# When the fp8 adjacency blocks of a two-layer graph kernel are made, and with which operations

## The chip, the cores and the metric

The kernel runs on one core of one Trainium2 chip. The metric is device microseconds (us) of one execution. The engines are TensorE (PE: matmuls, and PEld: its weight loads), VectorE (DVE), ScalarE (ACT), GpSimd (POOL) and SyncE (SP, which here only issues DMAs). Each takes its own instructions in the order in which they were written, and waits where an operand isn't there yet.

## The reference, cut to what matters

`x` is 3327 x 512 and `adj` is 3327 x 3327 with entries 0 and 1, both in float32.

```
# layer 0: two attention layers over the graph
for l in range(2):
    Wh, Ws = split(x @ W[l])                      # 512 columns each
    a      = softmax(Wh @ Ws.T, axis=-1) * adj
    x      = leaky_relu(a @ Wh + x, 0.01)
x = layernorm(x_in + x)
# layer 1: a binary linear layer, gathered over the graph
xw  = max(sign(x), 0) @ sign(weight).T            # small integers
out = layernorm(x + relu(adj @ xw))
```

So `adj` is used three times: as a mask in each of the two attention layers, and as the left operand of the last product `adj @ xw` (the aggregation). For that last product the kernel keeps `adj` in fp8 blocks that it makes on the way, while the mask is in SBUF anyway.

## The kernel before, in words

**Tiling.** The 3327 rows are padded to 26 tiles of 128, or 13 pairs (NQ = 13). A step is a pair (g, q): 256 target rows by 256 source rows, 169 steps per attention layer. All big products are done on 2 x 2 quarters with seven multiplications instead of eight, which needs sums of quarters.

**Scores.** The scores are made for 512 targets and 256 sources at a time: a unit is (c, q), made in two halves, `ahead` lists the halves. A unit is seven products in the order Z1, X2, Z6, Y5 (first half) and Z7, Y3, Z4 (second half), each two float32 matmuls of 128x256 (L586). ACT copies Z1, Z6, Y5, Z7 (p1, u2, p5, u3; L603) and Z4 (L638) out of PSUM; DVE adds (L613 after X2, L628 after Z7, L634 after Y3) and keeps a running maximum (L654, L656). The three PSUM banks of the scores go round: in the built program a unit's Z1 takes the bank that L613 of the unit before has read, its X2 mostly the one that L634 has read, its Y5 then the one that L638 has read. For the last pair of targets (c = 6, one half only) there are plain products instead (`direct`, L643).

**Attention steps.** The loop `for v in range(-LOOK - 4, len(steps))` with LOOK = 30 writes the whole order of the work down. In iteration v stand: half-unit v + 30 of the scores; for step v + 3 the shift by the column maximum (L739, DVE) and the exponential (L744, L745, ACT); for step v + 2 the running sum (L750) and the mask, `masked` (L755, DVE), then four sums of quarters on POOL (L793 to L796); for step v the seven products with the values (`values`, L820). Inside an iteration every piece of work carries a number from about 0 to 1, and the pieces are written in the order of these numbers. So iterations up to v = -4 hold scores alone, from v = 0 on PE alternates scores and values, and after v = 151 there are values alone. When a group g is done, `take_out` and `finish` (L846 to L928) follow over the next steps. Around v = -4, and later in the last third of each odd group, stands `column_max` (L687 to L707), which turns the running maxima into the shift `off` that L739 needs.

**Blocks.** `load_adj` brings a 256 x 256 float32 mask (256 KB, tag `adj`, 4 buffers) on SP's queue, in the iteration four before its step; where the mask has padding, POOL clears that first (L719, L721), and SP's load waits for it. For half of the steps in each attention layer, those with q of the layer's parity, the mask is also made into seven fp8 blocks of 128 x 128 (tile `ab`, tag `adj_b`, 2 buffers): three plain quarters and the four sums S1 to S4 of quarters. In iteration k - 2 of a step k, DVE makes the sums (`halved_sums`, L775), ACT casts the plain quarters (`halved`, L761 and L762), DVE tests that every entry is 0 or 1 (`exact`, L784, in place); an iteration later POOL issues the store to DRAM (`keep_blocks`, L778). Which mask is made in which iteration is set by the dictionary `blocks`: steps of groups 0 to 8 in their own iteration, the 28 (layer 0) or 24 (layer 1) steps of groups 9 to 12 spread over iterations of the other parity of groups 0 to 8, each with a second load of its mask.

**Aggregation.** At the end `load_aggregate` reads the blocks back and `aggregate` (L1134) multiplies them; `BLOCKS` says which of the seven is used by which product.

Of the kernel before, what the change touches and what calls it, by code (L numbers as in the profile page):

```python
# [15 lines left out]
ALU = mybir.AluOpType  # L16
# [3 lines left out]
P = 128  # L20
# [10 lines left out]
def kernel(  # L31
# [8 lines left out]
    nc = tc.nc  # L40
    N, D = x.shape
    L = w_stack.shape[0]
# [4 lines left out]
    NQ = NT // 2  # L47
    assert NT % 2 == 0 and D == 4 * P

    def rows(t):  # L50
        return min(P, N - t * P)
# [11 lines left out]
    def half_cols(g):  # L63

        return g * HW, min(HW, N - g * HW)
# [9 lines left out]
    LOOK = 2 * NQ + 4  # L75
# [14 lines left out]
    cnt = keep.tile([P, NQ * NQ], F32, name="cnt")  # L90
# [13 lines left out]
    adj_d = tc.dram_tile([NQ, P, NQ, 7, P], F8, name="adj_d")  # L104
# [5 lines left out]
    def load_rows(eng, dst, src, r):  # L110

        cut = r - r % 16
        engines = eng if isinstance(eng, tuple) else (eng,)
        if cut:
            engines[0].dma_start(out=dst[:cut], in_=src[:cut])
        if cut < r:
            engines[-1].dma_start(out=dst[cut:r], in_=src[cut:r])
# [437 lines left out]
    def attention(l, att):  # L555
# [3 lines left out]
        steps = [(g, q) for g in range(NQ) for q in range(NQ)]  # L559
        ahead = [(c, q, s) for c in range(NC) for q in range(NQ) for s in range(2)]  # L560
        sc, top, total, off, adj, acc, gs, xs, ch = ({} for _ in range(9))
# [152 lines left out]
        def load_adj(g, q):  # L714
            i0, n = half_cols(g)
            at = att.tile([P, 2, HW], F32, tag="adj", bufs=4, name=f"adj_{l}_{g}_{q}")
            adj[g, q] = at
            if n < HW:
                nc.gpsimd.memset(at[:, :, n:], 0.0)  # L719
            if rows(2 * q + 1) < P:  # L720
                nc.gpsimd.memset(at[:, 1], 0.0)  # L721
            if rows(2 * q + 1) == P:
                nc.sync.dma_start(
                    out=at[:, :, :n],
                    in_=adjT[2 * q * P : (2 * q + 2) * P, i0 : i0 + n].rearrange(
                        "(a p) i -> p a i", p=P
                    ),
                )
                return
            for a in range(2):  # L730
                j = 2 * q + a
                load_rows(
                    nc.sync, at[:, a, :n],
                    adjT[j * P : j * P + rows(j), i0 : i0 + n], rows(j),
                )

        def shift(g, q):
            s = sc[g, q]
            nc.vector.tensor_tensor(s, s, off[g].to_broadcast([P, 2, HW]), ALU.subtract)  # L739

        def exponential(g, q):
            if q == 0:
                total[g] = att.tile([P, 2, HW], F32, tag="total", name=f"total_{l}_{g}")
                nc.scalar.activation(total[g], sc[g, q], AF.Exp)  # L744
            nc.scalar.activation(sc[g, q], sc[g, q], AF.Exp)  # L745

        def running(g, q):

            if q > 0:
                nc.vector.tensor_tensor(total[g], total[g], sc[g, q], ALU.add)  # L750

        def masked(g, q):

            s = sc[g, q]
            nc.vector.tensor_tensor(s, s, adj[g, q], ALU.mult)  # L755
            sums(g, q, s)

        def halved(g, q):

            at, t = adj[g, q], adj[g, q, "b"]  # L760
            nc.scalar.copy(t[:, 0:2], at[:, :, :P], saturate=False)  # L761
            nc.scalar.copy(t[:, 2], at[:, 1, P:], saturate=False)  # L762

        def halved_sums(g, q):
            at = adj[g, q]
            t = adj[g, q, "b"] = att.tile(
                [P, 7, P], F8, tag="adj_b", bufs=2, name=f"ab_{l}_{g}_{q}"
            )
            a11, a21, a12, a22 = (at[:, k, ts(i, P)] for k in range(2) for i in range(2))
            s1, s2, s3, s4 = (t[:, i] for i in range(3, 7))  # L770
            for to, a, b, op in (
                (s1, a21, a22, ALU.add), (s2, s1, a11, ALU.subtract),
                (s3, a11, a21, ALU.subtract), (s4, a12, s2, ALU.subtract),
            ):
                nc.vector.tensor_tensor(to, a, b, op, saturate=False)  # L775

        def keep_blocks(g, q):
            nc.gpsimd.dma_start(out=adj_d[g][:, q], in_=adj.pop((g, q, "b")))  # L778

        def exact(g, q):  # L780

            at = adj.pop((g, q))
            i = g * NQ + q
            nc.vector.scalar_tensor_tensor(  # L784
                at, at, 0.0, at, ALU.is_gt, ALU.not_equal, accum_out=cnt[:, i : i + 1],
            )

        def sums(g, q, s):
# [10 lines left out]
        def load_ws(g, q):  # L799
            t = att.tile([P, 4, HD], F32, tag="ws", bufs=WS, name=f"ws_{l}_{g}_{q}")  # L800
            nc.sync.dma_start(out=t, in_=ws_d[l][q])
            ws[g, q] = t
# [150 lines left out]
        else:  # L953
# [3 lines left out]
            for i in range(2 * KD):  # L957
                h, t = divmod(i, KD)
# [11 lines left out]
            n = len(steps) - end - 3  # L970
# [19 lines left out]
            laid, n = [], len(steps)  # L990
# [6 lines left out]
                early.setdefault(end + 7 + i, []).append((0.65, lambda: parts.pop(0)()))  # L997


        first = NQ * (NQ - 4)  # L1000
        mine = [i for i, e in enumerate(steps) if e[1] % L == l]
        room = [i for i, e in enumerate(steps[:first]) if e[1] % L != l][2:]
        late = [i for i in mine if i >= first]
        blocks = {i: steps[i] for i in mine if i < first}
        blocks.update(
            {room[n * len(room) // len(late)]: steps[i] for n, i in enumerate(late)}
        )
        later, after = [], []
        first_products = NQ * NQ - EARLY
        for v in range(-LOOK - 4, len(steps)):  # L1010
            u = v + LOOK

            if 0 <= v + WS - 1 < len(steps):
                load_ws(*steps[v + WS - 1])
            if 0 <= v + 4 < len(steps):
                load_adj(*steps[v + 4])
                if blocks.get(v + 4, steps[v + 4]) != steps[v + 4]:
                    load_adj(*blocks[v + 4])
            for lead, load in ((2, load_xs), (4, load_gs)):
                if 0 <= u + lead < len(ahead):  # L1020
                    c, q, h = ahead[u + lead]
                    if h == 0 and (lead == 2 or q == 0):
                        load(c, q)
            work, after = after, []
            if 0 <= v + 3 < len(steps):
                s3 = steps[v + 3]
                work += [(0.0, lambda: shift(*s3)), (0.12, lambda: exponential(*s3))]
            if 0 <= v + 2 < len(steps):
                s2 = steps[v + 2]
                work += [(0.01, lambda: running(*s2)), (0.4, lambda: masked(*s2))]  # L1030
                of = blocks.get(v + 2)
                if of:
                    work += [
                        (0.6, lambda: halved_sums(*of)), (0.62, lambda: exact(*of)),
                        (0.61, lambda: halved(*of)),
                    ]
                    after.append((0.5, lambda of=of: keep_blocks(*of)))
            if later:
                work += [(0.7, later.pop(0))]
            if 0 <= u < len(ahead):  # L1040
                work += scores(*ahead[u])
            if v >= 0:
                work += values(*steps[v])
            work += early.get(v, [])
            if last and 0 <= v - first_products < EARLY:
                p = v - first_products
                work += [(0.5, lambda i=i: aggregate(0, 0, p, i)) for i in BANKS[0]]
            for _, do in sorted(work, key=lambda e: e[0]):
                do()
            if v >= 0 and steps[v][1] == NQ - 1:  # L1050
                later += finish(steps[v][0])
            if last:
                load_products(v)
# [26 lines left out]
    EARLY = NQ - 2  # L1080
    XH = NT // 2
    BANKS = (0, 1), (2, 3), (4, 5), (6,)
    BLOCKS = 0, 1, 4, 5, 3, 6, 2
    xw, xw_tiles, xt, ah, po = {}, [], {}, {}, {}

    def load_products(v):
# [37 lines left out]
    def aggregate(g, b, p, i):  # L1124
        if p == 0 and i == BANKS[b][0]:
            pool, tag = (ps_acc, "acc") if g % 2 else (ps_ch, "ch") if b < 3 else (ps_tr, "tr")
            po[g, b] = pool.tile([P, 2, HD], F32, tag=tag, name=f"agg_{g}_{b}")
        x1, x2, t = xw[2 * p], xw[2 * p + 1], xt.get(p)
        if i < 2:
            of = (x1, x2)[i][:, :HD]  # L1130
        else:
            of = (t[:, 1], t[:, 2], t[:, 0], x2[:, HD:], t[:, 3])[i - 2]

        nc.tensor.matmul(  # L1134
            po[g, b][:, i % 2], ah[g, p][:, BLOCKS[i]], of,
            start=(p == 0 and i % 2 == 0), stop=(p == NQ - 1), skip_group_check=True,
        )
# [223 lines left out]
```

## Time and profile before

| what | value |
|---|---|
| median of 3 runs | 2616.8 us (2616.53 to 2617.85) |
| the profiled execution: time | 2613.73 us |
| its span, first to last instruction | 2611.9 us |
| PE busy | 2578.8 us, 99% of the span |
| PEld busy | 2234.7 us, 86% |
| DVE busy | 2109.5 us, 81% |
| POOL busy | 1091.7 us, 42% |
| ACT busy | 799.8 us, 31% |
| mean granted clock of TensorE | 0.999 |
| the scores' products into bank Z (L586), both layers: first and last start | 184.7 us, 2276.3 us |
| the products with the values (L820), both layers: first and last start | 276.6 us, 2471.0 us |

How to read it: "busy" is the time in which an engine has an instruction under way; a matmul's end is modelled, so that a short stall of PE can hide between two matmuls. The table of stretches gives, for each stretch, an engine's busy time and in brackets how many of its instructions fall into it; where all matmuls are alike, too low a count shows a stall better than the busy time does. A group line of the profile reads: line, engine, operation, names out<-in, partitions x elements and type, count | busy us, mean ns of one | idle time just before them and what ended it. A line of waits reads: who, at which line, waited for whom: us in total, times, longest.

### The profile page before, as it was taken

How to read it: one execution, taken by the hardware profiler on the slowest of the kernel's cores; microseconds unless marked ns; L12 is line 12 of the kernel's file. 1: busy time of each engine (PE TensorE's matmuls, PEld its weight loads, DVE VectorE, ACT ScalarE, POOL GpSimd, SP SyncE). 2: the span in 40 equal slices, each digit the busy share in tenths (PEclk: the TensorE clock that was granted, in tenths of full speed). 3: DMA queues.
4: the chain of work that ended last, by engine and by line, in shares of the span. 5: the costliest groups of instructions: out<-in, count | busy, mean ns of one | idle time of the engine just before them, and what ended most of it. 6: DMA issues, size and time to landing. Idle time of an engine off the chain costs nothing. (4 is left out here: it accounts for less than half of the span.)

```text
span 2611.9 us, 40070 instructions
## 1 busy us (share of the span) xinstructions
PE 2578.8 (99%) x12511; PEld 2234.7 (86%) x12536; DVE 2109.5 (81%) x4422; ACT 799.8 (31%) x1978; POOL 1091.7 (42%) x2025
## 2 busy tenths in 40 slices
PE   9999999999999999999999999999999999999998
PEld 7888888888888888887888888888888888888787
DVE  6754888899888996768874689989899898777976
ACT  3323332333323332221332333333333333222143
POOL 3640343444434444456662044444444444454610
PEclk9999999999999999999999999999999999999999
DMA  6855777777777877698865678777787777678775
GB/s 216 293 193 180 241 241 265 241 268 251 261 240 236 276 239 237 223 265 252 300 242 179 224 225 283 249 250 258 239 281 247 246 263 237 231 260 262 262 252 182
DMA packets 309783, 639.15 MB, mean 245 GB/s; under 512 B 35048, under 2 KB 177986, under 8 KB 308027
## 3 DMA queue, kind: packets, MB, share of 16 engines
q1 hardware_dynamic: 273868, 530.29, 62.8%
q0 software_dynamic: 35664, 106.18, 11.0%
q8 instruction: 103, 1.69, 0.3%
q14 instruction: 118, 0.96, 0.1%
q10 hardware_dynamic: 30, 0.03, 0.0%
HBM read 529.69 MB, written 106.67 MB: 244 GB/s over the span
## 5 line engine op out<-in xcount | busy, mean ns | idle before, releaser
L586 PE MATMUL pZ<-gs,xs 128*128 128x256 f32 x2496 | 636.9, 379 | 3.0 <-ACT u L603 2.8
L793 POOL TENSOR_TENSOR as<-s 128x128 f32<-128x128 f32 x338 | 162.7, 481 | 1052.6 <-DVE s L755 873.2
L586 PEld LDWEIGHTS pZ<-gs,xs 128*128 128x128 f32 x2496 | 473.0, 190 | 71.3 <-ACT u L603 6.3
L820 PE MATMUL acc<-ws,s 128*128 128x256 f32 x1352 | 402.4, 379 | 0.1
L820 PE MATMUL acc<-wh,s 128*128 128x256 f32 x1352 | 355.7, 379 | 0.7 <-DVE s L755 0.4
L820 PE MATMUL acc<-ws,as 128*128 128x256 f32 x1352 | 348.0, 380 | 4.2 <-POOL as L795 4.1
L745 ACT ACTIVATE s<-s 128x512 f32<-128x512 f32 x338 | 213.2, 631 | 394.3 <-DVE s L739 393.3
L586 PE MATMUL pY<-gs,xs 128*128 128x256 f32 x1248 | 320.8, 379 | 6.0 <-ACT p L603 6.0
L820 PEld LDWEIGHTS acc<-ws,as 128*128 128x128 f32 x1352 | 256.1, 190 | 45.7 <-POOL as L795 8.6
L820 PEld LDWEIGHTS acc<-wh,s 128*128 128x128 f32 x1352 | 256.6, 190 | 36.7 <-DVE s L755 1.9
L820 PEld LDWEIGHTS acc<-ws,s 128*128 128x128 f32 x1352 | 255.7, 190 | 35.5 <-DVE h L855 1.3
L586 PEld LDWEIGHTS pY<-gs,xs 128*128 128x128 f32 x1248 | 236.6, 190 | 40.0 <-ACT p L603 7.9
L656 DVE TENSOR_TENSOR top<-top,s 128x512 f32<-128x512 f32 x286 | 199.9, 713 | 72.9 <-ACT s L643 52.6
L739 DVE TENSOR_TENSOR s<-s,off 128x512 f32<-128x512 f32 x338 | 246.8, 730 | 0.6
L755 DVE TENSOR_TENSOR s<-s,adj 128x512 f32<-128x512 f32 x338 | 239.5, 709 | 8.6 <-DMA adj<-in_adjT_dram 0.6
L750 DVE TENSOR_TENSOR total<-total,s 128x512 f32<-128x512 f32 x312 | 230.3, 738 | 0.0
L795 POOL TENSOR_TENSOR as<-s 128x128 f32<-128x128 f32 x338 | 202.1, 598 | 26.5
L603 ACT COPY u<-pZ 128x256 f32<-128x256 f32 x312 | 115.5, 370 | 308.0 <-PE pZ L586 304.9
L820 PE MATMUL acc<-wh,as 128*128 128x256 f32 x676 | 202.5, 381 | 0.0
L794 POOL TENSOR_TENSOR s<-s 128x128 f32<-128x128 f32 x338 | 182.9, 541 | 27.4
L796 POOL TENSOR_TENSOR as<-s,as 128x128 f32<-128x128 f32 x338 | 183.0, 541 | 26.5
L628 DVE TENSOR_TENSOR s<-p,u 128x256 f32<-128x256 f32 x156 | 66.5, 427 | 137.6 <-ACT u L603 136.9
(214 smaller groups left out, 3886.8 us busy)
## 6 DMA issues: line engine op xcount, KB each, us to landing
ws<-ws_d SPq DMA_DIRECT2D x338, 512.0 KB, 3.8
xs<-xs_d SPq DMA_DIRECT2D x182, 512.0 KB, 5.7
adj<-in_adjT_dram SPq DMA_DIRECT2D x324, 256.0 KB, 4.3
xs<-xs_d SPq DMA_DIRECT2D x156, 384.0 KB, 6.2
gs_d<-gsp POOLq DMA_DIRECT2D x88, 256.0 KB, 3.1
gs<-gs_d SPq DMA_DIRECT2D x12, 1792.0 KB, 10.9
adj_d<-ab POOLq DMA_DIRECT2D x169, 112.0 KB, 3.9
ahl<-adj_d SPq DMA_DIRECT2D x78, 224.0 KB, 5.0
```

The costliest lines, as they stand in the source:

```text
L586: nc.tensor.matmul(ch[bank], xs[c, q, a][:, k], gs[c][:, b, k], start=(start and k == 0), stop=(k == 1), skip_group_check=True,)
L603: nc.scalar.copy(ch[name], ch[bank])
L656: nc.vector.tensor_tensor(top[i], top[i], t, ALU.max)
L739: nc.vector.tensor_tensor(s, s, off[g].to_broadcast([P, 2, HW]), ALU.subtract)
L745: nc.scalar.activation(sc[g, q], sc[g, q], AF.Exp)
L750: nc.vector.tensor_tensor(total[g], total[g], sc[g, q], ALU.add)
L755: nc.vector.tensor_tensor(s, s, adj[g, q], ALU.mult)
L793: nc.gpsimd.tensor_tensor(s3, a11, a21, ALU.subtract)
L794: nc.gpsimd.tensor_tensor(a21, a21, a22, ALU.add)
L795: nc.gpsimd.tensor_tensor(s2, a21, a11, ALU.subtract)
L796: nc.gpsimd.tensor_tensor(s4, a12, s2, ALU.subtract)
L820: nc.tensor.matmul(acc[g][i // 2][:, i % 2], a[i], b[i], start=(q == 0 and i % 2 == 0), stop=(q == NQ - 1), skip_group_check=True,)
```

## The change

The blocks of a step are made with other operations, at another place in the loop, and for some steps in other iterations.

- **Sums.** `halved_sums` (four DVE operations on 128 columns, two of which read or write fp8 intermediates) becomes `block_sums`, three DVE operations: the difference of the left and right halves, for both rows of quarters at once and in place in the float32 mask (L770 of the new kernel); S2 from it (L771); S4 and S1 side by side as one sum of 256 columns (L774). They read float32 alone.
- **Test.** `exact` (L790) comes ahead of the sums, and writes its unused result into four of the fp8 blocks instead of over the mask.
- **ACT.** `raw_blocks` (L765) casts two quarters an iteration earlier than before (k - 3). The other two blocks, S3 and the fourth quarter, are cast by ACT in `keep_blocks` (L782), an iteration after the sums (k - 1), just ahead of the store (L783).
- **Place.** 14 steps of each attention layer are moved into iterations of scores alone: into v + 2 = -27, -25, ..., -1. In layer 0 these are the steps (12, q) and (11, q) with even q; in layer 1 the steps (g, 11) of odd g, and (12, q) and two of (11, q). All others are made at their own step, those of groups 9 to 11 too, and no iteration makes blocks of two parities any more. The masks of the moved steps are loaded a second time (28 loads instead of 52).
- The order of the seven blocks in memory changes, and `BLOCKS` with it.

```diff
-        def halved(g, q):
-
-            at, t = adj[g, q], adj[g, q, "b"]
-            nc.scalar.copy(t[:, 0:2], at[:, :, :P], saturate=False)
-            nc.scalar.copy(t[:, 2], at[:, 1, P:], saturate=False)
-
-        def halved_sums(g, q):
-            at = adj[g, q]
+        def raw_blocks(g, q):
             t = adj[g, q, "b"] = att.tile(
                 [P, 7, P], F8, tag="adj_b", bufs=2, name=f"ab_{l}_{g}_{q}"
             )
-            a11, a21, a12, a22 = (at[:, k, ts(i, P)] for k in range(2) for i in range(2))
-            s1, s2, s3, s4 = (t[:, i] for i in range(3, 7))
-            for to, a, b, op in (
-                (s1, a21, a22, ALU.add), (s2, s1, a11, ALU.subtract),
-                (s3, a11, a21, ALU.subtract), (s4, a12, s2, ALU.subtract),
-            ):
-                nc.vector.tensor_tensor(to, a, b, op, saturate=False)
+            nc.scalar.copy(t[:, 0:2], adj[g, q][:, :, :P], saturate=False)
+
+        def block_sums(g, q):
+            at, t = adj[g, q], adj[g, q, "b"]
+            left, right = at[:, :, :P], at[:, :, P:]
+            nc.vector.tensor_tensor(left, left, right, ALU.subtract)
+            nc.vector.tensor_tensor(
+                t[:, 6], at[:, 1, P:], at[:, 0, :P], ALU.subtract, saturate=False
+            )
+            nc.vector.tensor_tensor(
+                t[:, 4:6].rearrange("p a i -> p (a i)"), at[:, 0], at[:, 1], ALU.add,
+                saturate=False,
+            )
 
         def keep_blocks(g, q):
-            nc.gpsimd.dma_start(out=adj_d[g][:, q], in_=adj.pop((g, q, "b")))
+            at, t = adj.pop((g, q)), adj.pop((g, q, "b"))
+            quarter = at.rearrange("p k (i n) -> p (k i) n", n=P)
+            nc.scalar.copy(t[:, 2:4], quarter[:, 0:4:3], saturate=False)
+            nc.gpsimd.dma_start(out=adj_d[g][:, q], in_=t)
 
         def exact(g, q):
 
-            at = adj.pop((g, q))
+            at = adj[g, q]
             i = g * NQ + q
+            junk = adj[g, q, "b"][:, 3:7].rearrange("p (k i) n -> p k (i n)", k=2)
             nc.vector.scalar_tensor_tensor(
-                at, at, 0.0, at, ALU.is_gt, ALU.not_equal, accum_out=cnt[:, i : i + 1],
+                junk, at, 0.0, at, ALU.is_gt, ALU.not_equal, accum_out=cnt[:, i : i + 1],
+                saturate=False,
             )
...
-        first = NQ * (NQ - 4)
+
         mine = [i for i, e in enumerate(steps) if e[1] % L == l]
-        room = [i for i, e in enumerate(steps[:first]) if e[1] % L != l][2:]
-        late = [i for i in mine if i >= first]
-        blocks = {i: steps[i] for i in mine if i < first}
-        blocks.update(
-            {room[n * len(room) // len(late)]: steps[i] for n, i in enumerate(late)}
-        )
+        alone = list(range(4 - LOOK, 1, 2))
+        moved = [i for i in mine if l and steps[i][1] == NQ - 2 and steps[i][0] % 2]
+        moved += [i for i in mine[::-1] if i not in moved][: len(alone) - len(moved)]
+        blocks = {i: steps[i] for i in mine if i not in moved}
+        blocks.update({i - 1: steps[j] for i, j in zip(alone, moved)})
...
             if 0 <= v + 4 < len(steps):
                 load_adj(*steps[v + 4])
-                if blocks.get(v + 4, steps[v + 4]) != steps[v + 4]:
-                    load_adj(*blocks[v + 4])
+            elif v + 4 in blocks:
+                load_adj(*blocks[v + 4])
...
-                of = blocks.get(v + 2)
-                if of:
-                    work += [
-                        (0.6, lambda: halved_sums(*of)), (0.62, lambda: exact(*of)),
-                        (0.61, lambda: halved(*of)),
-                    ]
-                    after.append((0.5, lambda of=of: keep_blocks(*of)))
+            if v + 3 in blocks:
+                work += [(0.61, lambda: raw_blocks(*blocks[v + 3]))]
+            if v + 2 in blocks:
+                of = blocks[v + 2]
+                work += [(0.6, lambda: exact(*of)), (0.62, lambda: block_sums(*of))]
+                after.append((0.4, lambda of=of: keep_blocks(*of)))
...
-    BLOCKS = 0, 1, 4, 5, 3, 6, 2
+    BLOCKS = 0, 1, 6, 2, 5, 4, 3
```

## The prediction, made before the changed kernel ran

> **What bounds the kernel now.** First the page's busy times and slices, then the stretches of 50 us, then the waits in the stretches where PE falls short, then the groups of the block work, last the order of time where the moved work will stand.
>
> ```profile
> PE 2578.8 (99%) x12511; PEld 2234.7 (86%) x12536; DVE 2109.5 (81%) x4422; ACT 799.8 (31%) x1978; POOL 1091.7 (42%) x2025
> ...
> PE   9999999999999999999999999999999999999998
> ...
> DVE  6754888899888996768874689989899898777976
> ```
>
> PE is the bound: 33.1 us of idle time in 2611.9 us. A change on DVE, ACT and DMA can only give back PE's stalls, or add some. The stretches say where they are:
>
> ```profile
> 350.00:400.00 50.00, 50.00 (x235) 43.98 (x234) 41.70 (x89) 15.12 (x40) 20.99 (x41) 1.00 0.81 278
> 400.00:450.00 50.00, 48.45 (x223) 41.41 (x222) 45.88 (x113) 15.54 (x44) 18.82 (x38) 1.00 0.72 233
> 450.00:500.00 50.00, 48.51 (x224) 42.05 (x223) 44.41 (x92) 15.18 (x40) 23.62 (x46) 1.00 0.75 242
> ...
> 750.00:800.00 50.00, 45.77 (x209) 38.81 (x208) 44.74 (x101) 14.76 (x40) 19.91 (x38) 1.00 0.69 222
> ```
>
> The first bracket counts PE's matmuls. Full stretches of layer 0 hold 233 to 235; in scores alone a unit of 28 matmuls takes 6.04 us (Z1 at 190.76 and at 196.80), 0.216 us each. Layer 0 loses 10.6 + 9.6 + 24.6 matmuls here and 1.6 in 600 to 650: 46.4 x 0.216 = **10.0 us** (busy time shows 7.4 of it). Layer 1's groups 0 to 8 show two waits of 0.6 us (near 1830 and 2150). Where values begin, 250 to 300 us is 6.6 matmuls short (1.4 us) and 1450 to 1500 7.6 (1.6 us). The end of layer 1 (2440 to 2470, PE waiting for L795) loses some 4 us, but holds no block work before or after the change. The waits from 430 to 432.2 us:
>
> ```profile
> ACT ab L761 <- DMA adj_d<-ab: 2.6, 1, 2.6
> DVE ab L775 <- DMA adj_d<-ab: 2.6, 1, 2.6
> PEld pY L586 <- ACT p L603: 1.9, 1, 1.9
> PE pY L586 <- ACT p L603: 1.5, 1, 1.5
> ```
>
> The cast L761 wants an `ab` buffer whose store, issued at 425.27, hasn't landed; behind it on ACT stands the copy p5, for which Y3 waits. The same stands at 458 and 779 us. So layer 0's stalls come from two blocks in neighbouring steps with two buffers, where `column_max` has made the first late. Over the kernel such waits are 28.6 us on DVE and 27.1 on ACT.
>
> **What the Trainium skill says.** "DMA: Bandwidth & Descriptors", section "Anatomy of one DMA — SWDGE (gpsimd) path": about 2.0 us fixed plus bytes by 436 GB/s, and a wait on a semaphore is taken by the issuing sequencer ahead of the transfer. For 112 KB that is an estimate of 2.3 us; this trace has a median of 3.9 and here about 5.9, so the trace is used. The second statement agrees: SP stands at one load with all later ones behind it. "VectorE: DVE Perf Modes", section "Mode 1× (REGULAR) — the baseline": one result a cycle, at 0.96 GHz; 256 columns are an estimate of 0.27 us, 128 of 0.13. The trace has 0.42 (L628) and 0.35, so some 0.15 to 0.2 us is fixed per operation, and fewer, wider ones save.
>
> **The change, part by part.** Block work, by form:
>
> ```profile
> L784 DVE SCALAR_TENSOR_TENSOR adj<-adj 128x512 f32<-128x512 f32 x169 | 139.8, 827 | 25.4 <-ACT ab L762 8.9 <-ACT u L603 0.5 <-DVE ab L775 0.5
> L775 DVE TENSOR_TENSOR ab<-adj 128x128 fp8e4<-128x128 f32 x338 | 118.0, 349 | 29.2 <-DMA adj_d<-ab 28.6 <-POOL as L793 0.4
> L775 DVE TENSOR_TENSOR ab<-adj,ab 128x128 fp8e4<-128x128 f32 x169 | 86.5, 512 | 0.0
> L775 DVE TENSOR_TENSOR ab<-ab,adj 128x128 fp8e4<-128x128 fp8e4 x169 | 79.3, 469 | 5.8
> ```
>
> *DVE per block.* Before: 2 x 0.349 + 0.512 + 0.469 + 0.827 + 0.078 (accumulator read) = 2.58 us. After: 0.42 (256 columns, L628's row) + 0.35 + 0.42 + 0.91 = 2.10. An fp8 result of 256 columns and a strided one in place are not in the trace: between 0.35 and 0.54 each, so 1.95 to 2.35; I take 2.1. ACT: 0.401 + 0.296 becomes 2 x 0.40, on an engine at 31%. Saved on DVE: 169 x 0.48 = 81 us, worth nothing by itself under PE.
>
> *(a) Stores.* Blocks now come two steps (12 us) apart, so a buffer is wanted again after 24 us; a store of 3.9 to 6 us is long done. Layer 0's 10.0 us go, and DVE in groups 0 to 8 falls from 90% to about 75% (in layer 0, 20.5 x 2.58 us per 26 steps of 6.05 us become 14 x 2.1). What is next: ACT's cast in `keep_blocks` waits for L770; from 0.62 of a step to 0.4 of the next are 4.7 us, less 1.3 for L790 and L770, so DVE may be 3 us late. I leave 0.8 us. **-9.2 us** (bounds -10.0 and -6). *(b)* Layer 1's two waits (exponential behind a late L739): **-1.2** (0 to -2.2).
>
> *(c) Start of layer 0's scores.* The first moved mask, (12, 12), is padded. SP has had the second unit's operands in early; now this mask stands ahead of them (they were ahead of the last input loads before). Its second piece waits for POOL's clearing, and POOL is busy with stores until 186.90:
>
> ```profile
> 186.36 0.54 POOL L417 DMA_DIRECT2D ws_d<-t  x1
> ```
>
> Clearing (0.11 + 0.32) to 187.4, issues of 0.38 each on SP, the last piece at 188.2, landing about 3 us later: 191.3. L765 stands between u2 and p5 on ACT: cast to 191.7, p5 to 192.1, and Y3, begun at 189.03 before, waits 3.1 us. The second unit's first operand (issued 188.6, landing 3.8 to 5 us) is needed at 193.9: covered, else more. **+3.1** (2.0 to 5). *(d)* Layer 1's first mask, (1, 11), isn't padded: issued at 1399.7 when PE leaves the buffer, landed at 1404, Y3 begins at 1404.85. **+0.3** (0 to 1.5).
>
> *(e) Scores alone.* Per unit of 6.04 us DVE has 3 x 0.42 + 2 x 0.71 + 2.1 = 4.8 us. Order: L634, block, two maxima, L613; the next Z1 wants that L613 some 2.5 us later. No stall; 896 KB and 256 KB per unit fit too.
>
> *(f) Where values begin* DVE has no gap from 262.21 on:
>
> ```profile
> 262.62 0.42 DVE L634 TENSOR_TENSOR s<-pY,u 128x256 f32<-128x256 f32 x1
> ...
> 268.74 0.69 DVE L739 TENSOR_TENSOR s<-s,off 128x512 f32<-128x512 f32 x1
> 269.35 0.42 DVE L628 TENSOR_TENSOR s<-p,u 128x256 f32<-128x256 f32 x1
> 269.68 0.42 DVE L634 TENSOR_TENSOR s<-pY,u 128x256 f32<-128x256 f32 x1
> ...
> 271.28 0.68 DVE L739 TENSOR_TENSOR s<-s,off 128x512 f32<-128x512 f32 x1
> ```
>
> The blocks (11, 2) and (11, 0) now come right behind the two L634. The first moves the second L634 to 272.2, and X2, which began at 270.19 on its release, waits 2.1 us. With the second, L739 of 271.28 is 4.2 us late, with it the exponential, then a cast (0.4) and u2 on ACT: Z7, at 273.17 before, begins at about 277.4. X2 of the next unit waits 0.7 us. In all 4.8 us instead of 1.4: **+3.4**. In layer 1, likewise with (11, 9) and (11, 7), 4.2 instead of 1.6: **+2.6**. Bounds of both together 3 to 8 us (the cheapest and dearest block, twice each).
>
> *(g) Groups 9 to 11* get 14 and 10 blocks that they had not. From v = 126 a step is 4.7 us; DVE has 26.2 us in 1050 to 1080 and gets 3 x 2.1: over 30 by 2.5 us, and slack follows (5.9 in 1080 to 1090). **+0.6** (0 to 4). (h) 24 loads fewer, the new order of blocks: 0, under the slack of SP's queue; with that cover gone 0.4 us of issue each.
>
> Sum: -9.2 - 1.2 + 3.1 + 0.3 + 3.4 + 2.6 + 0.6 = **-0.4 us**: 2613.7 becomes 2613.3 in the profiled execution. That execution lies 3.1 us under the median of the runs, so 2616.4.
>
> **The rivals.** *R1, faster:* (a) and (b) as above, but the starts cost half or less, because landings in (c) come at the short end and PE regains at one place what it lost at another (waits in (f) overlap instead of adding): -10.4 + 3 = -7.4, 2609.4. For it: 55 us of waits on stores go; against: DVE's unbroken row from 262 us. *R2, slower:* ACT's cast in `keep_blocks` becomes the wait. Where DVE is more than 3 us behind its place, the cast blocks u2 or p5 as L761 did; at some 8 places (ends of odd groups, group 10) by 1 us: -0.4 + 8, 2624.4. It decides from 3 us of lateness; for it, (g)'s full stretches and L745's waits of up to 5.9 us for L739; against, DVE at 75%. *R3:* the change doesn't do what it says: stalls stay, since late DVE and not the stores made them, and the starts cost: 2626. Against it: the named waits.
>
> **How the numbers follow.** Forecast 0.45, R1 0.38, R2 0.14, R3 0.03. A measurement of this kernel can tell 0.2%, 5.2 us: faster 0.38, same 0.45, slower 0.17. The forecast's own range is 2611.6 to 2622. For 8 in 10 the range goes to 2606.5 (a fifth of R1 is left out, 0.08) and 2623 (over half of R2 and R3, 0.10).
>
> **What would show it.** Right: matmul counts of 233 and more around 430, 455 and 775 us, no waits on `adj_d<-ab`; a gap of PE near 189 us behind the cast; 2 + 2 us on X2 and Z7 near 272; DVE busy lower by about 80 us. Wrong: no gap at those starts (R1), or PE waiting for p5 or u2 behind the second cast of ACT (R2), or stalls still near 430 (R3).

## The result, and the profile after

The changed kernel takes 2622.4 us (median of 15 runs, 2617.9 to 2624.9), the kernel before 2615.7 us in the same series (15 runs, 2612.0 to 2617.9): a ratio of 1.0025, interval 1.0019 to 1.0032. It is slower by 0.25%, 6.7 us, where 2616.4 was forecast. The time lies 0.4 us above the forecast's own range (2611.6 to 2622) and inside the wider one (2606.5 to 2623), but the sum of the prediction (-0.4 us) is wrong by 7 us: the kernel was to stay where it was, and it got slower.

First the page's busy times of the changed kernel, then its stretches of 50 us at the places that the prediction named. The columns are PE, PEld, DVE, ACT and POOL (busy us, and number of instructions), granted clock, DMA share, GB/s.

```profile
PE 2584.1 (99%) x12536; PEld 2240.1 (85%) x12536; DVE 2110.5 (81%) x4253; ACT 813.7 (31%) x1978; POOL 1186.0 (45%) x2023
```

```profile
150.00:200.00 50.00, 47.61 (x213) 41.27 (x212) 27.48 (x63) 13.16 (x36) 20.94 (x39) 0.97 0.62 211
...
250.00:300.00 50.00, 43.79 (x198) 36.92 (x197) 39.93 (x101) 18.13 (x50) 10.88 (x18) 1.00 0.75 253
...
400.00:450.00 50.00, 50.00 (x233) 44.03 (x232) 43.92 (x98) 16.83 (x42) 23.31 (x40) 1.00 0.77 267
450.00:500.00 50.00, 50.00 (x234) 43.99 (x233) 40.98 (x76) 14.59 (x37) 23.70 (x42) 1.00 0.72 232
...
750.00:800.00 50.00, 50.00 (x234) 43.98 (x234) 44.62 (x92) 15.08 (x39) 24.24 (x42) 1.00 0.70 233
...
1450.00:1500.00 50.00, 45.70 (x201) 38.59 (x200) 36.63 (x96) 19.29 (x54) 4.13 (x11) 0.97 0.78 262
```

The stalls on stores are gone: 233 or 234 matmuls near 430, 460 and 780 us, where 223, 224 and 209 stood. The starts pay for it: against full stretches of 233, 20 matmuls are missing where layer 0's scores begin, 35 where its values begin (6 of them before the change too), and 32 where layer 1's values begin (7 of them before too). And there is something new in the last columns: a granted clock of 0.97 in two of these stretches.

**Stages.** Since ACT's copies out of PSUM stand in the same order in all these kernels, one and the same copy can be looked up in two traces, and the growth of the difference between its two start times tells in which stage time was lost. The next table does that for every kernel of this study, as us lost (+) or gained (-) against the trace before; the head of a column gives its stage in the time of the kernel before. What is left out (204 to 258) is 0.0 to 0.2 in all. Each row comes from one execution; stages that an edit does not touch differ by up to 0.9 us from row to row.

| kernel | 0 to 12 | 12 to 204: scores begin, layer 0 | 258 to 338: values begin | 338 to 1040: groups 0 to 8 | 1040 to 1268: groups 9 to 12 | 1268 to 1468: scores begin, layer 1 | 1468 to 1542: values begin | 1542 to 2266: groups 0 to 8 | 2266 to 2469 |
|---|---|---|---|---|---|---|---|---|---|
| changed | 2.61 | 4.35 | 6.02 | -10.65 | 0.83 | 0.55 | 7.06 | -1.74 | 0.28 |
| e1, mask ahead | 1.84 | 5.25 | 4.15 | -10.65 | 1.18 | 0.51 | 4.59 | -1.74 | 0.24 |
| e2, first whole | 1.59 | 0.51 | 6.44 | -10.65 | 0.84 | 0.53 | 7.09 | -1.74 | 0.24 |
| e3, twelve | 0.40 | 3.60 | 0.47 | -10.65 | 1.12 | 0.63 | 0.23 | -1.74 | 0.96 |
| e4, whole and twelve | 1.49 | 0.61 | 0.70 | -10.65 | 0.85 | 0.82 | 0.23 | -1.74 | 0.94 |
| e5, before with three | 1.42 | 0.00 | 0.01 | -8.90 | -0.51 | -0.20 | 0.01 | 0.40 | 0.02 |
| e6, late cast | 1.99 | 4.32 | 4.35 | -10.65 | 1.32 | 0.35 | 4.86 | -1.74 | 0.25 |
| e7, old operations | 2.43 | 5.11 | 4.31 | -10.65 | 3.59 | 0.33 | 3.65 | -1.74 | 0.30 |
| e8, own step | 0.65 | 0.00 | 0.53 | -10.65 | 8.84 | 0.00 | 0.21 | -1.74 | 12.15 |
| e9, both masks | 0.11 | 0.39 | 4.58 | -10.65 | 0.84 | 0.50 | 5.31 | -1.74 | 0.25 |
| e10, mixed | 3.25 | 0.00 | 0.01 | -8.92 | -0.51 | 0.30 | 0.01 | -1.74 | 1.48 |

The first column is the same program in all of them. It differs from launch to launch, and in the trace of before it was the shortest of all; that is why the two profiled executions lie 9.4 us apart (span 2621.3 against 2611.9) and the medians 6.7. The other columns of the first row add up to +6.7.

**Where scores begin.** What was waited for between 186 and 198 us in the changed kernel (who, at which line, for whom: us, times, longest), then PE's order of time there:

```profile
ACT ab L765 <- DMA adj<-in_adjT_dram: 3.0, 1, 3.0
PEld pY L586 <- ACT p L603: 2.8, 1, 2.8
```

```profile
190.79 1.03 PE L586 MATMUL pZ<-gs,xs 128*128 128x256 f32 x4
194.20 1.74 PE L586 MATMUL pY<-gs,xs 128*128 128x256 f32 x4 [2.39 <-ACT p L603]
195.74 2.58 PE L586 MATMUL pZ<-gs,xs 128*128 128x256 f32 x6
```

The chain is the one that was predicted: POOL's clearing, the mask, the cast L765, p5, Y3. But four matmuls then take 1.74 us instead of 1.03: the clock record shows half speed from 194.6 for 3.41 us (a half clock, in what follows). That loses another 1.7 us, half of 3.41.

**Where values begin.** SP's order of time before layer 0's values, the cast on ACT that it leads to, and PE's waits behind it:

```profile
258.71 0.42 SPq L568 DMA_DIRECT2D gs<-gs_d  x1
259.25 0.38 SPq L723 DMA_DIRECT2D adj<-in_adjT_dram  x1
```

```profile
269.74 0.40 ACT L765 CAST ab<-adj 128x256 fp8e4<-128x256 f32 x1 [2.33 <-DMA adj<-in_adjT_dram]
270.05 0.36 ACT L603 COPY p<-pY 128x256 f32<-128x256 f32 x1
```

```profile
270.47 1.13 PE L586 MATMUL pY<-gs,xs 128*128 128x256 f32 x4 [1.79 <-ACT p L603]
...
280.91 1.13 PE L586 MATMUL pX<-gs,xs 128*128 128x256 f32 x4 [1.54 <-DVE s L634]
...
285.73 1.13 PE L586 MATMUL pZ<-gs,xs 128*128 128x256 f32 x4 [1.33 <-ACT u L603]
```

The mask of key -3 (a key is the iteration that `blocks` gives to a block: its sums are made at v + 2 = -3) is issued half a microsecond behind the operands of the second group of columns, 1792 KB that take 10.3 us themselves, and lands, that is, has all arrived, 10.4 us after its issue (the page's median for a mask is 4.1). p5 stands behind the cast, and Y3 on PE waits 1.79 us. The waits of X2 for L634 and of Z7 for u2, some 10 and 15 us later, are the ones that step (f) foresaw. In layer 1 the same pair is issued at 1471.5 and 1472.0; the cast waits 3.1 us for it, PE 2.56, and a half clock follows. Over the whole kernel ACT waited for masks at L765 four times, 8.8 us; for the cast L782, the rival R2, it never waited:

```profile
L765 ACT CAST ab<-adj 128x256 fp8e4<-128x256 f32 x169 | 68.4, 405 | 8.8 <-DMA adj<-in_adjT_dram 8.8
L782 ACT CAST ab<-adj 128x256 fp8e4<-128x256 f32 x169 | 66.5, 394 | 0.0
```

### The profile page after: what moved, and what is told of

The parts are those of the page before. It is cut to its first block, busy times and chain, and to the rows that moved or that the text cites. A ratio compares the mean times of both kernels' runs of the same rounds, so it can differ in the third digit from the quotient of the medians.

```text
span 2621.3 us, 39707 instructions
## 1 busy us (share of the span) xinstructions
PE 2584.1 (99%) x12536; PEld 2240.1 (85%) x12536; DVE 2110.5 (81%) x4253; ACT 813.7 (31%) x1978; POOL 1186.0 (45%) x2023
## 5 line engine op out<-in xcount | busy, mean ns | idle before, releaser
L800 POOL TENSOR_TENSOR as<-s 128x128 f32<-128x128 f32 x338 | 185.8, 550 | 404.5 <-DVE s L755 302.0
L783 POOL DMA_DIRECT2D adj_d<-ab x169 | 92.4, 547 | 576.5 <-ACT ab L782 330.2
L656 DVE TENSOR_TENSOR top<-top,s 128x512 f32<-128x512 f32 x286 | 224.7, 800 | 56.0 <-ACT s L638 36.4
L739 DVE TENSOR_TENSOR s<-s,off 128x512 f32<-128x512 f32 x338 | 254.2, 752 | 0.6
L801 POOL TENSOR_TENSOR s<-s 128x128 f32<-128x128 f32 x338 | 226.0, 669 | 27.0
L803 POOL TENSOR_TENSOR as<-s,as 128x128 f32<-128x128 f32 x338 | 210.6, 623 | 26.5
L802 POOL TENSOR_TENSOR as<-s 128x128 f32<-128x128 f32 x338 | 203.4, 602 | 26.5
```

The lines of the kernel that those rows point to most:

```text
L656: nc.vector.tensor_tensor(top[i], top[i], t, ALU.max)
L800: nc.gpsimd.tensor_tensor(s3, a11, a21, ALU.subtract)
L801: nc.gpsimd.tensor_tensor(a21, a21, a22, ALU.add)
L802: nc.gpsimd.tensor_tensor(s2, a21, a11, ALU.subtract)
L803: nc.gpsimd.tensor_tensor(s4, a12, s2, ALU.subtract)
```

## The experiments

Ratios are to the kernel before, from runs beside it; the changed kernel has 1.0025. 0.001 is 2.6 us. "DVE's row" is its unbroken run of work where values begin.

**Two masks.** Does the late landing of two masks make the loss, or does DVE's full row hide it? First (e1) the mask of key -3, loaded ahead of the operands:

```diff
             elif v + 4 in blocks and v != -7:
                 load_adj(*blocks[v + 4])
+                if v == -9:
+                    load_adj(*blocks[-3])
```

> One edit to the changed kernel: the mask of the block step at key -3 is loaded two iterations earlier, ahead of the 1.75 MB operand load (gs) for the second group of columns instead of behind it. Theory L (landing): the early cast on ACT (L765) waits for that mask, which lands over 10 us after its issue since the operand load is ahead of it in the queue; p5 and Y3 wait behind the cast, 2.2 us in layer 0 and 2.9 us plus a half-clock stretch of 3.4 us (1.7 us lost) in layer 1. Then both gaps go, and the half clock of layer 1 with them: 2622.4 - 2.1 - 4.4, some 2616. Theory D (full row of DVE): the row of block operations and column maxima where values begin sets the end there, and the landing hides under it: 2621 to 2622.5, with the gap moved to X2 or Z7 a few us later.

Measured: 2617.6 us, ratio 1.0010 (1.0004 to 1.0017): 3.9 us less than the changed kernel, where theory L said 6.5 and theory D at most 1. The gap of Y3 is gone in layer 0 and 0.67 us between starts (of which 0.22 is the matmul) in layer 1. Of the 2.1 and 4.4 us, 1.9 and 2.5 came back (table): part of it is taken up by DVE's row behind. Both theories hold a share. Layer 1's half clock is gone, but one appears in layer 0, at 281.08, behind X2's wait of 1.50 us for L634. It cost little: Z7's wait for u2, 1.33 us in the changed kernel, is missing behind it. (The start of its scores, which the edit leaves alone, took 0.9 us more than in the trace of the changed kernel.)

Then (e2) the first mask of layer 0, without padding:

```diff
+        if l == 0:
+            moved[0], moved[8] = moved[8], moved[0]
         blocks = {i: steps[i] for i in mine if i not in moved}
```

> One edit to the changed kernel: in layer 0 the first moved step and the ninth change places, so that the first mask has no padding (no clearing by POOL, one DMA instead of three). Theory L: SP need not wait for POOL, the mask is issued 3 to 4 us earlier and lands when p5 is due; the gap of 2.8 us before the first unit's second Y3 falls to 0.5 or less and no half clock follows it: 2622.4 - 2.3 - 1.7, some 2618.4. Rival (the second load's place in the queue alone makes the gap, whatever the mask): gap 2 us or more, 2621 to 2622.5.

Measured: 2617.5 us, ratio 1.0008 (1.0000 to 1.0016), 4.4 us less, as theory L had it. SP issues this mask at 185.64 and the second unit's operands at 186.09, and the stage costs 0.51 us instead of 4.35. No half clock follows there. Where layer 1's values begin it stays (1479.86), and in layer 0's there is one at 278.36 that the trace of the changed kernel does not have; again Z7's wait is missing behind it.

**Fewer moved steps (e3).** Nothing where the values begin:

```diff
-        alone = list(range(4 - LOOK, 1, 2))
+        alone = list(range(4 - LOOK, -3, 2))
```

> One edit to the changed kernel: 12 steps are moved instead of 14, into keys -27 to -5; the last two of the list are made at their own step. No block stands near the iterations where values begin. Theory L and D together (both landing and full row of DVE cost there): all of the 6.3 us (layer 0) and 7.0 us (layer 1) that the changed kernel lost there come back, 2622.4 - 13.3, some 2609. If the landing alone counted, what the run with the mask ahead of the operand load gives, some 2616, is the floor.

Measured: 2612.3 us, ratio 0.9989 (0.9983 to 0.9996): 9.4 us less. In the table 5.6 and 6.8 us of the two starts of values come back, 12.4 in all; the ratios, each known to some 2 us, show less of it. The floor of 2616 that the landing alone would give is passed. No half clock is in this trace up to the end of the kernel, so the start of the scores, which keeps its padded mask, costs 3.60 instead of 4.35.

With the whole first mask as well (e4):

> The edits of the two runs before together (first mask without padding in layer 0; 12 moved steps). If the losses are separate and add: 2622.4 - 4.0 - 13.3, some 2605, which is below the kernel before by its three store stalls. If PE finds another stall in their place, 2609 to 2613.

Measured: 2608.3 us, ratio 0.9975 (0.9964 to 0.9986), faster than both kernels, than the one before by 0.25%. In the table the losses were separate and add: the starts now cost 0.61, 0.70 and 0.23. The time lies 3 us above the 2605 that was expected, which is about what the interval leaves open.

**Landing against DVE's row (e9).** All 14 steps moved, both masks mended:

> The changed kernel, still with 14 moved steps, with both edits to its loads: the first mask of layer 0 without padding, and the mask at key -3 loaded ahead of the operand load. If the two landings are separate losses, they add: 1.0025 - 0.0017 - 0.0015, a ratio of some 0.9993 (2613.5). What then still lies between it and the run with 12 moved steps and a whole first mask (0.9975) is DVE's row where values begin: 4 to 5 us. If instead DVE's row sets the end once the landings are mended (its gaps grow by what the landings gave back): 1.0005 or more.

Measured: 2614.1 us, ratio 0.9995 (0.9987 to 1.0003), as the sum of the two had it. What still stands between it and e4 (0.9975), 5.2 us by the ratios and 3.9 + 5.1 by the table, comes from the two blocks that are made where values begin. These are PE's waits from 268 to 286 us:

```profile
PE pX L586 <- DVE s L634: 1.3, 1, 1.3
PE pZ L586 <- ACT u L603: 1.3, 1, 1.3
PE pX L586 <- ACT s L638: 1.2, 1, 1.2
```

X2 waits for L634, Z7 for u2, the next X2 for a copy of ACT: the places of step (f), after the masks no longer matter. But not all that is left is DVE's row. In layer 1, from 1464 to 1478 us:

```profile
ACT ab L765 <- DMA adj_d<-ab: 1.5, 1, 1.5
PE pY L586 <- ACT p L603: 1.0, 1, 1.0
```

With its mask there in time, the cast waits for a block buffer instead. Among scores alone blocks come 6 us apart, not 12, and the store of the second block before, issued at 1465.02, takes 8.72 us to land beside the 1792 KB of operands issued at 1463.57. In layer 0 the same cast waits 0.9 us and PE 0.3. No run has this placement with a third buffer.

**The cast itself (e6).** The same loads, the cast L765 an iteration later:

```diff
-            if v + 3 in blocks:
-                work += [(0.61, lambda: raw_blocks(*blocks[v + 3]))]
             if v + 2 in blocks:
                 of = blocks[v + 2]
-                work += [(0.6, lambda: exact(*of)), (0.62, lambda: block_sums(*of))]
+                work += [
+                    (0.595, lambda: raw_blocks(*of)), (0.6, lambda: exact(*of)),
+                    (0.62, lambda: block_sums(*of)),
+                ]
```

> The changed kernel with one edit: the first cast of ACT (L765) stands an iteration later (k - 2, just ahead of the test) instead of k - 3; the same 14 steps are moved, the same masks loaded at the same places. Theory L: the mask has one iteration (3 us among scores alone) more to land, so the three gaps of Y3 (2.8, 2.2 and 2.9 us) fall below 0.5 and the half clock with them: 2621.5 - 4.3 - 2.1 - 4, some 2611 to 2613; what is left of the loss is DVE's row (2 to 4 us in each layer). Rival: the cast only moves the wait to DVE's test, which stands ahead of the maxima and L613: 2619 or more.

Measured: 2618.5 us, ratio 1.0010 (1.0004 to 1.0017). At both starts of values this gives as much as loading the mask earlier (4.35 and 4.86 against 4.15 and 4.59 us), less than theory L had it: Y3's wait is gone, but in its place Z1 waits, 1.4 us in layer 0 behind the block sums on DVE (L770 by the profile), much as the rival had it, and 1.5 us in layer 1 for its operands. Where the scores begin nothing is gained (4.32 against 4.35), and there theory L failed. PE's order of time in this run:

```profile
191.88 1.03 PE L586 MATMUL pZ<-gs,xs 128*128 128x256 f32 x4
195.31 1.41 PE L586 MATMUL pZ<-gs,xs 128*128 128x256 f32 x4 [2.40 <-DMA xs<-xs_d]
```

Y3 no longer waits, but the second unit's Z1 does, for its operands: SP issued them at 190.89, behind the three pieces of the padded mask; in the kernel before, the first of these loads was issued at 188.37. So the padded first mask costs twice, once through the cast and once through the queue behind it, and the later of the two shows. A half clock follows here too, at 195.96. The prediction had called the operands covered, "else more".

**The operations (e7).** The old sums and casts (four DVE sums, both casts at k - 2, the old order of blocks) in the new places:

> The changed kernel's placement of the steps (14 moved) with the block operations of the kernel before: four sums on 128 columns, the casts at k - 2, no cast at k - 1. Theory L: the mask is wanted an iteration later, so the landing gaps vanish as with the late cast, while DVE's row where values begin grows by 0.5 us a block, four blocks in each layer: 2613 to 2616. Rival (the new operations bring a gain of their own that offsets part of the loss): 2622 or more.

Measured: 2619.8 us, ratio 1.0012 (1.0005 to 1.0019), not to be told from the late cast, and above what was expected, mostly by the start of the scores (5.11) and groups 9 to 12 (3.59). Only in groups 9 to 12 of layer 0 do the new operations help (1.32 with the late cast against 3.59). The -10.65 is there with the old operations too: it is the spacing of the blocks that gives it.

**Stores (e5).** The kernel before, with one edit:

```diff
-                [P, 7, P], F8, tag="adj_b", bufs=2, name=f"ab_{l}_{g}_{q}"
+                [P, 7, P], F8, tag="adj_b", bufs=3 - l, name=f"ab_{l}_{g}_{q}"
```

> The kernel before with one edit: three buffers for the blocks (adj_b) in layer 0, two in layer 1 as before. Theory S (stores): layer 0's stalls near 430, 457 and 779 us come from the buffer whose store has not landed; a third buffer takes them away with all else as it was: 2615 - 10, some 2605 to 2606. Theory D' (DVE late behind the column maxima makes them, the store is only named): 2613 to 2615, stalls moved by less than a microsecond.

Measured: 2605.8 us, ratio 0.9964 (0.9952 to 0.9976). Its stretches at the three stalls:

```profile
400.00:450.00 50.00, 50.00 (x235) 43.98 (x234) 45.63 (x111) 16.32 (x43) 20.32 (x41) 1.00 0.75 245
450.00:500.00 50.00, 49.95 (x232) 43.65 (x231) 46.26 (x93) 16.34 (x42) 23.16 (x45) 1.00 0.77 255
750.00:800.00 50.00, 49.87 (x233) 43.55 (x232) 48.19 (x99) 15.99 (x42) 23.62 (x46) 1.00 0.75 252
```

The named waits were the cause, and 896 bytes per partition end them with nothing moved. DVE is no less busy than before (48.2 of 50 us at the third stall, where it had 44.7): theory D' falls.

**What moving is worth (e8).** The new operations, and no step moved:

```diff
-        alone = list(range(4 - LOOK, 1, 2))
-        moved = [i for i in mine if l and steps[i][1] == NQ - 2 and steps[i][0] % 2]
-        moved += [i for i in mine[::-1] if i not in moved][: len(alone) - len(moved)]
+        alone, moved = [], []
```

> The changed kernel with no step moved: all blocks, groups 9 to 12 too, are made at their own step with the new operations; no second loads of masks. The losses at both starts vanish (2621.5 - 17.5 = 2604), and the blocks of groups 11 and 12 fall into stretches where a step is 4.7 us and DVE has 42 of 50 us: 7 more blocks of 2.1 us in each of two groups per layer. If DVE's slack takes them in: 2604 to 2607; if PE waits for it for half of their time (some 15 us a layer over what groups 9 and 10 cost): 2615 or more.

Measured: 2625.7 us, ratio 1.0044 (1.0031 to 1.0058): the second case. The starts cost 0.5 us or less, and the last groups 8.84 us in layer 0 and 12.15 in layer 1, 1.7 of these by a half clock at 2467.72. The -10.65 is there with no step moved, so it needs neither the moving nor the new operations, only that no iteration of groups 0 to 8 makes a block of the other parity. What PE waited for from 2410 to 2470 us there:

```profile
PEld acc L827 <- POOL as L802: 12.8, 9, 2.6
PE acc L827 <- POOL as L802: 8.9, 9, 2.2
```

And what POOL waited for in the same stretch:

```profile
POOL adj_d L783 <- ACT ab L765: 8.0, 4, 3.2
POOL adj_d L783 <- ACT ab L782: 4.8, 1, 4.8
```

POOL stands mostly at the store of a block, for which ACT's casts are late, and the sums that PE wants are queued behind it. So with these operations the blocks of groups 11 and 12 do have to go elsewhere; both kernels do that, and the kernel before pays no start for it.

**A mixture (e10).** Layer 0 as in e5, and in layer 1 twelve steps moved as in e3, with the old operations:

> The kernel before with three block buffers in layer 0, and in layer 1 twelve steps moved into keys -27 to -5 with the old operations. Layer 0 gives 9.6 us as with three buffers alone; layer 1 loses its two waits of 0.6 us near 1830 and 2150 and gains the price of its start (up to 0.7) and of blocks in groups 9 to 11 (up to 1.5): 2604 to 2607, not to be told from three buffers alone. If moving the blocks is worth something in layer 1 by itself: 2602 or less.

Measured: 2606.4 us, ratio 0.9965 (0.9951 to 0.9979), not to be told from e5. The two waits of layer 1 go (-1.74), and its start and its end give as much back.

**The clock (e11).** In e5's kernel, waits of chosen length, made by idle copies of ACT between u2 and p5:

```diff
+        holds = dict(zip((-26, -22, -18, -14, -10), ((6, 8, 10, 12, 14), (7, 9, 11, 13, 15))[l]))
+        def hold(n):
+            for _ in range(n):
+                nc.scalar.copy(scr, ident)
...
+            if v in holds:
+                work += [(0.61, lambda: hold(holds[v]))]
```

> The kernel before with three block buffers in layer 0, and with idle copies of ACT (6, 8, 10, 12, 14 in layer 0, 7, 9, 11, 13, 15 in layer 1, of a 128x128 tile into a scratch tile) between u2 and p5 of five half-units of scores alone in each layer: each makes Y3 wait, by 0.5 to 4 us, longer with each. Theory C: TensorE's clock is halved for 3.41 us where it stood idle for about 2 us or more within one of the 3.41 us stretches that the clock record is cut into: no half clock after the short holds, one after each long one, 1.7 us lost. Rival: the two half clocks of the changed kernel have nothing to do with its gaps (they come with the kernel's load or time): half clocks at other places, or none.

Measured (one execution, 2644.0 us, which is not a time to compare): two of the ten holds on PE, the second and third of layer 0:

```profile
218.04 1.13 PE L586 MATMUL pY<-gs,xs 128*128 128x256 f32 x4 [1.56 <-ACT p L603]
219.00 1.89 PE L586 MATMUL pZ<-gs,xs 128*128 128x256 f32 x8
...
232.60 1.36 PE L586 MATMUL pY<-gs,xs 128*128 128x256 f32 x4 [2.21 <-ACT p L603]
233.75 3.39 PE L586 MATMUL pZ<-gs,xs 128*128 128x256 f32 x8
```

After the wait of 1.56 us eight matmuls take 1.89 us, after that of 2.21 us 3.39. PE's ten waits were 0.90 to 3.86 us long. The four up to 1.89 us had no half clock behind them, the six from 2.21 us one each, as theory C had it, and there was none elsewhere before the end of the kernel. So the half clocks come from PE's own gaps; the last section gives the rule that fits.

## Why the prediction was wrong

- **(a) -9.2 and (b) -1.2** were right, and too careful: -10.65 and -1.74. e5 shows the cause of 8.9 us of it, the store; the rest comes with the wider spacing (e7, e8). The 0.8 us kept back for the cast in `keep_blocks` was not needed. DVE's share in groups 0 to 8 fell less than was said, in layer 0 from 88% to 83% (340 to 1040 us) and not from 90% to 75%.
- **(c) +3.1**: right in chain and size (2.4 us of wait) as far as it goes; 1.7 us of half clock were not in it, so 4.35. e6 shows a second path of the same length, the operands, that the step took for covered.
- **(d) +0.3, (e) 0, (g) +0.6**: 0.55, 0.0 and 1.1 (0.83 and 0.28 in the two layers).
- **(f) +3.4 and +2.6 is the step that failed**: 6.02 and 7.06. Its term for DVE's row was not too small: the waits that it foresaw, of X2 and Z7, add up to 4.4 us in the changed kernel's layer 0 (1.54 + 0.36 + 1.33 + 1.18) and 2.4 in layer 1 (1.64 + 0.74), where it had 4.8 and 4.2. What the step had at nothing is the landing. It looked at DVE's row and took the masks as there, since in scores alone "896 KB and 256 KB per unit fit too". At this place SP's queue holds 1792 KB more, and the mask directly behind it is the one that a cast ahead of p5 needs: Y3 waits 1.79 and 2.56 us, and in layer 1 a half clock follows. Loading that mask earlier (e9 against the changed kernel) gives back only 1.4 and 1.8 us of this. The rest goes to other waits that then show: X2's wait of 1.35 us in layer 1, which the changed kernel does not show, and the cast's wait for a store.
- **DVE busy lower by about 80 us** failed: 2110.5 against 2109.5. A block does cost less, but 2.24 us (781 + 80 + 525 + 406 + 447 ns) and not 2.10: 58 us are saved, and as much comes back in other groups whose instructions grew longer. No run shows what that cost; PE is the bound over most of the kernel, but where values begin DVE's row sets the time.
- **The rivals.** R1 (cheap starts) fell: they cost more. R2 had the sign, and its 2624.4 lies nearest to the time, but by luck: L782, the cast that it feared, waited 0.0 us. R3 fell with the first three stretches. A rival with the landing of a moved load behind a large one was not among them.

By the table, 12.4 us are gained where 10.4 were forecast, and the starts and groups 9 to 12 cost 19.1 (4.35 + 6.02 + 0.83 + 0.55 + 7.06 + 0.28) where 10.0 were: 2.0 us better and 9.1 worse. Mending the two masks gives back 7.8 us by the ratios (e9), taking the last two steps away from the start of the values 5.2 more (e4 against e9). The best kernels, e5 and e10, don't make the change in layer 0 at all.

## What to carry to other kernels

When work that reads a load is moved, look up what is issued just ahead of that load in its queue, in the place where it will stand, and take the landing there and not the median; and look up what follows it in the queue. Before rearranging work around a wait for a buffer, price one more buffer: here it gave some 9 of the 12.4 us of gain and none of the loss. An instruction that waits for memory is best not put ahead of the copies that feed the engine which bounds the kernel; but putting it behind them (e6) moved a part of the wait instead of ending it.

## What the runs showed of the hardware

**A gap costs more than its length.** The clock record is cut into stretches of 3.41 us; all its changes lie a whole number of them apart (for instance 184.32 and 81.92 us). The Trainium skill, "TensorE: Matmul & The Clock Gate", section "What's actually happening", tells of such a free-running window of 3413 ns, and its table says that the clock falls to half after an idle window. The runs agree on the window and show that less is enough. I laid PE's gaps (start to start, less 0.22 us, counted above 0.3 us) over these stretches in the traces of all kernels here. Up to 2560 us, where the end of the kernel begins, each of the 15 stretches in which PE stood idle for 1.97 us or more was followed by one at half clock, and none with 1.84 us or less was. A gap of 2.73 us in e3 was parted between two stretches (1.78 and 0.95 us, 1.58 with a smaller gap behind) and had none; one of 2.38 in e2 (1.05 and 1.33) the same. So whether a gap of 2 to 3.5 us is followed by a half clock also depends on where it falls, and that differs from launch to launch. The price of a half clock is up to 1.7 us: in e1 and e2, where another wait would have come anyway, it took that wait's place.

**The same operations got longer.** POOL's four sums took 541 ns on average before and 611 in the changed kernel, with no change to them; the maximum on DVE (L656) went from 713 to 800 ns. With the old operations in the new places (e7) POOL is busy 1115.6 us, with the new ones 1186.0, before 1091.7. So it comes mostly with the new operations, which read float32 alone; how, no run here shows.
